# Layer norm 1 of the third batch applied as two rows to an already transposed x, and its Q products placed two blocks later

## The chip, the cores and the metric

The kernel runs on one core of a Trainium2 chip. The core has five engines with a queue of instructions each, executed in order: TensorE (PE, matrix products), VectorE (DVE), ScalarE (ACT), GpSimd (POOL) and SyncE (SP, which here only issues DMAs). They wait for one another through semaphores. The metric is the time of one execution on the device in microseconds (us); lower is better. Everything is float32.

## The reference

One transformer block with cross attention, for 4 batches of 512 query rows, 512 context rows, width 512, 16 heads of 32, and an MLP of width 2048. For each batch:

```
x  = layer_norm(hidden, ln1_w, ln1_b)                  # layer norm 1
q  = x @ q_w + q_b;  k = ctx @ k_w + k_b;  v = ctx @ v_w + v_b
a  = softmax(q k^T / sqrt(32), masked)  (per head)
h  = (a v) @ cproj_w + cproj_b + hidden
y  = layer_norm(h, ln2_w, ln2_b)                       # layer norm 2
out = h + gelu(y @ fc_w + fc_b) @ proj_w + proj_b
layer_norm(x, w, b) = (x - mean) * rsqrt(var + 1e-5) * w + b
```

The change concerns layer norm 1 of batch 2 (of batches 0 to 3) and the q products of its first two groups of heads.

## The kernel before

**Units and blocks.** The work on attention is cut into 16 units: unit w is batch w // 4 and four heads, group w % 4. A unit takes two blocks, one for each half of its query rows, so there are 32 blocks, p = 0 to 31, and block p belongs to unit p // 2. Batch 2 is units 8 to 11 and blocks 16 to 23. A block (`block`) has on PE the scores of its 256 query rows (L317), on DVE the mask and the row minimum of the scores (`soften`, L323), on ACT the exponential (L327), on DVE the 32x32 transposes of the result (`turn`, L335). Then comes the *exchange*: POOL copies the diagonal parts (L393, four copies) and SP issues twelve DMAs for the others (L398), into one buffer pT. The product with v (`attend`, L415) reads pT; DVE then multiplies by the reciprocal sums (L420), which frees pT for the exchange of the next block. From block 10 on, `attend` of block p - 2 stands at the start of block p, so each exchange has about one block to finish.

**Fills.** PE would be idle during a block's softmax, so other work is written into each block by hand: `put(p, ...)` lists it in order. `fill(0)`, `fill(1)` and `fill(2)` take pieces from the list at three places of a block, with a cost of 3.4 for a product over four chunks (K: `prep_k` L255; Q: `prep_q` L267; V: `prep_v` L278; output projection: `cproj` L455) and 0.0 for pieces that use no PE. A list given as `mid` is emitted in the middle of the block, between the softmax steps of its two 128-row halves. `some(2)` takes the next products of the MLP of batch 0, which starts in block 11. The order written there is the order on every engine; nothing reorders it.

**Layer norm 1, two ways.** For batches 0 and 2, x is loaded by rows (`load_x`), DVE takes the statistics (L129, L130), POOL works out the reciprocal deviations (`ln_rs`, L135 to L148), ACT normalizes for batch 2 (L153, key in `NORM_ACT`), PE transposes 16 blocks of 128x128 (`ln_turn`, L166), and ACT applies weight and bias while it moves the result from PSUM into `xT` (L171). For batches 1 and 3 (`BY_ROW`), the host supplies x transposed as well (`rawT`). The statistics come from x by rows as before, but the factor rs and the offset -mean * rs are turned into two rows: `store_rn` transposes a small tile on DVE (L203) and writes it to DRAM (four DMAs, L206), `load_rn` reads both rows back, spread over all partitions (two DMAs, L213), `ln1_rows` applies them to the transposed x on POOL (a multiply and an add for each of four 128x512 tiles, L218), and `ln1_affine` applies weight and bias on ACT into `xT` (L222).

**What stands around the change.** Block 9 has the output projection of batch 0 (`c`), with the statistics of layer norm 2 of batch 0 (`stat`) and its `ln_rs`. Block 10 normalizes it (`norm`; rows t = 0, 1, 2 on ACT, L153, and t = 3 on DVE, L157) and transposes it (`t2`, `ln2_turn`, L166). Block 11 has the first MLP product (`fc_seven`, L646). `fc_sums` makes weight sums for the MLP on POOL (four operations, L597 and L600, and two DMAs that POOL issues, L689 and L690), for one pair of weight tiles at a time; it stands in block 10 and, from p = 11 on, after `attend` at each block's start, and runs ahead of the products by at most two pairs. `pb_` adds a bias row on POOL (L426, four operations), `v_bias` another (L309).

Of the kernel before, what the change touches and what calls it, by code (L numbers as in the profile page):

```python
# [12 lines left out]
F32 = mybir.dt.float32  # L13
# [7 lines left out]
P = 128  # L21
# [14 lines left out]
IN_G = (1, 3, 5, 7)  # L36
IN_XE = (25, 27, 29, 31)

BY_ROW = ((1, 1), (1, 3))
BY_ACT = ((1, 2),)  # L40
NORM_ACT = BY_ACT + ((2, 0), (2, 1))
MW = 8
WARM = 9
PW = 2 * NT * HG * HD
# [7 lines left out]
def xattn_block(ctx: ExitStack, tc: tile.TileContext, x, rawT, encT, mask, q_w, k_w, v_w, c_w, fc_w, p_w, vecs, rows, out):  # L52
# [108 lines left out]
    def ln_turn(key, d, xn, dst):  # L161

        w, bi = (LN1W, LN1B) if key[0] == 1 else (LN2W, LN2B)
        tp = acc_tile(f"tp{key[0]}_{key[1]}_{d}")
        for t in range(NT):
            nc.tensor.transpose(tp[:, ts(t, P)], xn[t][:, ts(d, P)], ident)  # L166
        wd, bd = vec[:, w + d : w + d + 1], vec[:, bi + d : bi + d + 1]
        if d in (1, 2) and key not in BY_ACT:
            nc.vector.tensor_scalar(dst[:, d, :], tp, wd, bd, ALU.mult, ALU.add)
        else:  # L170
            nc.scalar.activation(dst[:, d, :], tp, AF.Identity, bias=bd, scale=wd)  # L171
# [23 lines left out]
            ln_rs((1, b))  # L195

    def load_raw(b):
        S["xn", b] = [tiles.tile([P, L], F32, tag="xn", name=f"raw_{b}_{d}") for d in range(ND)]
        for d in range(ND):
            nc.sync.dma_start(out=S["xn", b][d], in_=rawT[b, ts(d, P), :])  # L200

# [474 lines left out]
    def raw_pair(b, c):  # L676
        return [S["fcw", b, 2 * c + i] for i in range(2)]

    def fc_sums():

        while count[3] < len(fc_pairs) and count[3] < count[4] + 2:
            b, c = fc_pairs[count[3]]
            if ("fcw", b, 2 * c + 1) not in S:
                return
# [284 lines left out]
    def do(fn):  # L969
        return [(0.0, fn)]  # L970
# [104 lines left out]
    def stat(b, *ts_):  # L1075
        return do(lambda: [stat2(b, t) for t in ts_])
# [6 lines left out]
    def put(p, *work, before=(), mid=()):  # L1083

        work = [item for part in work for item in part]
        ahead[p], mids[p] = list(before), list(mid)
        fills[p] = work
# [15 lines left out]
    c, t2 = C(0), turns2(0)  # L1103
    put(7, [v6, k], cb(0))
    put(8, x1, [q, v], x4)
    put(9, c[:1], do(lambda: attend(3, 1)), x2[:2], c[1:2], x2[2:], stat(0, 0), c[2:3], stat(0, 1),
        c[3:], stat(0, 2), x3, stat(0, 3), rs(0))
    k, q, v = A(8)
    put(10, [k], norm(0, 0, 1), [v], norm(0, 2, 3), do(fc_sums), [q], t2)
    k, q, v = A(9)  # L1110
    put(11, [k, v], some(2), pb_(0), mid=do(lambda: y_sums(0)))

    x1, x2, x3, x4 = inputs(3)
    put(12, [q], some(2))
    k, q, v = A(10)
    put(13, [k], some(2))
    put(14, [q], some(2), x1)
    put(15, x2[:1], V(10), x2[1:2], do(lambda: load_raw(3)), some(2), do(lambda: store_rn(3)), some(1),
        do(lambda: load_rn(3)), some(1))
# [108 lines left out]
```

## Time and profile before

| what | us |
|---|---|
| median of 3 runs (lowest to highest) | 761.14 (760.96 to 763.58) |
| the profiled execution | 766.39 |
| its span, from first to last instruction | 764.3 |
| PE, busy | 757.5 (99%) |
| DVE, busy | 602.0 (79%) |
| ACT, busy | 337.1 (44%) |
| POOL, busy | 334.7 (44%) |

The profiled execution is 5.25 us longer than the median; 2.09 us of it lie outside the span. A line of the timeline has the start, the duration, engine, source line, operation, output and inputs, the count of instructions merged into it, and in brackets the idle time before it with what ended it. One product of the program over 512 columns shows as two MATMUL instructions.

### The profile page before, as it was taken

The page shows a single profiled execution, that of the slowest core. Times are in us where ns is not written, and L with a number is a line of the kernel's source. Part 1 is how long each engine was busy: PE and PEld are TensorE (multiplying, and loading weights), DVE is VectorE, ACT ScalarE, POOL GpSimd, SP SyncE. Part 2 cuts the span into 40 slices and gives each one's busy share as a digit, 9 for nine tenths or more (in the row PEclk, how much of TensorE's full clock was granted, in tenths as well). Part 3 has the DMA queues.
Part 4 walks back from the last instruction along what each step waited for, and adds up shares of the span by engine and source line. Part 5 has one row for each costly group of instructions (what it writes and reads, how often), then busy time and mean ns, then how long its engine had stood idle before and what let it go on. Part 6 is the DMA issues. An engine that isn't in the chain of part 4 may idle for free.

```text
span 764.3 us, 12899 instructions
## 1 busy us (share of the span) xinstructions
PE 757.5 (99%) x4370; PEld 518.7 (68%) x4370; DVE 602.0 (79%) x1198; ACT 337.1 (44%) x766; POOL 334.7 (44%) x350
## 2 busy tenths in 40 slices
PE   9999999999989999999999999999999999999998
PEld 6655555566565545475464566458888899988997
DVE  3888999879976777887888889958877886747762
ACT  2566766565863475647753467501202221021200
POOL 1539447368653883443584444532060004303152
PEclk9999999999999999999999999999999999999999
DMA  8999889467796686765666867776724402146001
GB/s 325 341 255 243 204 207 254 111 199 196 214 251 212 194 242 169 184 184 130 167 141 179 212 194 197 171 226 212 270 97 131 163 31 90 36 133 218 1 15 42
DMA packets 60577, 134.59 MB, mean 176 GB/s; under 512 B 11312, under 2 KB 17072, under 8 KB 60384
## 3 DMA queue, kind: packets, MB, share of 16 engines
q1 hardware_dynamic: 58448, 126.73, 58.0%
q0 software_dynamic: 1920, 7.01, 2.8%
q8 instruction: 35, 0.57, 0.3%
q14 instruction: 30, 0.25, 0.1%
q10 hardware_dynamic: 144, 0.02, 0.0%
HBM read 69.23 MB, written 11.02 MB: 105 GB/s over the span
## 4 chain that ended last, share of the span: by engine, by line
PE 98%; SPq 1%; DMA 1%; issue 0%; DVE 0%; POOL 0%; POOLq 0%; DVEq 0%
PE q L646 25%; PE accp L705 11%; PE r L790 8%; PE sc L317 8%; PE av L415 8%; PE acck L255 7%; PE accq L267 7%; PE accc L455 6%; PE accv L278 5%; PE accv L298 3%; PE q1p L844 2%; PE q4p L826 2%; PE tp L166 1%; SPq L398 1%; DMA ptt<-q_w_dram 1%; PE warm L1023 1%
## 5 line engine op out<-in xcount | busy, mean ns | idle before, releaser
L327 ACT ACTIVATE ptt<-ptt,mn 128x512 f32<-128x512 f32 x256 | 181.7, 711 | 147.6 <-DVE mn L323 147.6
L323 DVE CUSTOM_DVE_ANT_0 ptt<-sc,mb 128x512 f32<-128x512 f32 x256 | 160.6, 682 | 20.1 <-PE sc L317 20.0
L335 DVE STREAM_TRANSPOSE tb<-ptt 128x1024 f32<-128x1024 f32 x128 | 153.3, 1217 | 1.0 <-ACT ptt L327 1.0
L393 POOL COPY pT<-tb 32x1088 f32<-32x1088 f32 x96 | 104.5, 1089 | 86.4 <-DMA pbt<-p_w_dram 28.0
L705 PE MATMUL accp<-pbt,gt 128*128 128x512 f32 x192 | 85.3, 596 | 0.0
L646 PE MATMUL q<-yT,gt 128*128 128x256 f32 x320 | 78.9, 380 | 0.0
L667 ACT ACTIVATE ga<-ga,vec 128x512 f32<-128x512 f32 x40 | 26.7, 714 | 93.3 <-DVE ga L600 83.5
L646 PEld LDWEIGHTS q<-yT,gt 128*128 128x128 f32 x320 | 61.0, 191 | 8.1
L705 PEld LDWEIGHTS accp<-pbt,gt 128*128 128x128 f32 x192 | 35.9, 190 | 44.6 <-issue 39.2
L317 PE MATMUL sc<-pbt 32*128 32x512 f32 x512 | 66.1, 621 | 0.0
L646 PE MATMUL q<-ys,gt 128*128 128x256 f32 x240 | 61.6, 380 | 0.0
L255 PE MATMUL acck<-xe,ptt 128*128 128x512 f32 x128 | 58.8, 603 | 0.2 <-issue 0.2
L267 PE MATMUL accq<-xe,ptt 128*128 128x512 f32 (+1 forms) x136 | 58.5, 575 | 0.0
L646 PEld LDWEIGHTS q<-ys,gt 128*128 128x128 f32 x240 | 45.7, 191 | 6.1
L600 DVE TENSOR_TENSOR ga<-q,ga 128x512 f32<-128x512 f32 (+1 forms) x60 | 36.2, 603 | 16.9 <-PE q L646 14.3
L415 PE MATMUL av<-pT,v 128*32 128x256 f32 x768 | 47.3, 387 | 2.0 <-DMA ptt<-q_w_dram 2.0
L327 ACT ACTIVATION_READ_ACCUMULATOR ptt<-ptt,mn 128x1 f32 x256 | 47.8, 187 | 0.0
L267 PEld LDWEIGHTS accq<-xe,ptt 128*128 128x128 f32 x136 | 24.9, 190 | 31.4 <-issue 23.0
L317 PEld LDWEIGHTS sc<-pbt 32*128 32x128 f32 x512 | 27.5, 187 | 26.0 <-issue 17.2
L255 PEld LDWEIGHTS acck<-xe,ptt 128*128 128x128 f32 x128 | 23.6, 192 | 31.2 <-issue 21.9
L455 PE MATMUL accc<-wc,oT 128*128 128x512 f32 x96 | 42.5, 598 | 0.0
L415 PEld LDWEIGHTS av<-pT,v 128*32 128x32 f32 x768 | 23.0, 111 | 26.2 <-issue 10.4
(219 smaller groups left out, 1265.4 us busy)
## 6 DMA issues: line engine op xcount, KB each, us to landing
pT<-tb SPq DMA_DIRECT2D x288, 136.0 KB, 2.4
pbt<-p_w_dram SPq DMA_DIRECT2D x40, 256.0 KB, 3.3
gt<-ws SPq DMA_DIRECT2D x20, 512.0 KB, 3.4
gt<-tb SPq DMA_DIRECT2D x48, 136.0 KB, 3.8
xe<-tb SPq DMA_DIRECT2D x48, 136.0 KB, 2.5
pbt<-fc_w_dram SPq DMA_DIRECT2D x24, 256.0 KB, 4.0
gt<-fc_w_dram SPq DMA_DIRECT2D x20, 256.0 KB, 3.2
ptt<-k_w_dram SPq DMA_DIRECT2D x16, 256.0 KB, 3.7
```

The lines of the kernel that those rows point to most:

```text
L255: nc.tensor.matmul(acc, S["wk", w][:, d, :], eT[:, d, :], start=(d == 0), stop=(d == ND - 1))
L267: nc.tensor.matmul(acc, S["wq", w][:, d, :], xT[:, d, c], start=(d == 0), stop=(d == ND - 1))
L317: nc.tensor.matmul(S["sc", w, qt][h], qT[r, ts(qt, P)], kT[r, :], start=True, stop=True)
L323: nc.vector.tensor_tensor_reduce(out=s, in0=S["sc", w, qt][h], in1=S["mb", w // NG], scale=1.0, scalar=FMAX, op0=ALU.add, op1=ALU.min, acc ...
L327: nc.scalar.activation(s, s, AF.Exp, bias=mn, scale=-1.0, accum_out=S["sums", w][:, qt, h : h + 1])
L335: nc.vector.transpose(tv[:, qt % 2, 2 * k : 2 * k + 2], S["ps", w, qt, k])
L393: nc.gpsimd.tensor_copy(pT[ts(i, HD), i], tb[ts(i, HD), i])
L415: nc.tensor.matmul(av[ts(h, HD), : 2 * P].rearrange(shape, **kw), v[:, t, ts(h, HD)], p[t][h], start=(t == 0), stop=(t == NT - 1),)
L455: nc.tensor.matmul(acc, S["oT", b][:, g, ts(t, P)], wc[:, g, :], start=(g == 0), stop=(g == NG - 1))
L646: nc.tensor.matmul(o, x[:, k], y[:, k], start=(k == 0), stop=(k == 1))
L705: nc.tensor.matmul(acc, gT[q % 2][:, k, ts(t, P)], S["pw", b, q * FQ + k], start=(k == 0), stop=(k == FQ - 1))
L790: nc.tensor.matmul(r, x[:, c], w[:, c], start=(c == 0), stop=(c == NP // 2 - 1))
```

## The change

Batch 2 joins `BY_ROW`: its x is loaded transposed as well, straight into `xT`, and the two rows and then weight and bias are applied there in place. The normalization on ACT, the 16 transposes on PE and the four moves from PSUM on ACT go away for batch 2. `load_raw(2)`, `store_rn(2)` and `load_rn(2)` stand in block 9; `ln1_rows(2, ...)` is split, tiles 0 and 1 in block 10 and tiles 2 and 3 in block 11, each time behind the copies of that block's exchange in POOL's queue; `ln1_affine(2)` ends block 11. Since `xT` is complete only then, Q of unit 8 moves from block 10 to block 12, and Q of unit 9 from block 12 to block 13. In block 10, `fc_sums` makes one pair instead of two (the second then comes at the start of block 11), the normalization of t = 0, 1 of layer norm 2 moves to the middle of the block, and that of t = 2, 3 ahead of V.

```diff
-BY_ROW = ((1, 1), (1, 3))
-BY_ACT = ((1, 2),)
-NORM_ACT = BY_ACT + ((2, 0), (2, 1))
+BY_ROW = ((1, 1), (1, 2), (1, 3))
+NORM_ACT = ((2, 0), (2, 1))
...
-        if d in (1, 2) and key not in BY_ACT:
+        if d in (1, 2):
...
     def load_raw(b):
-        S["xn", b] = [tiles.tile([P, L], F32, tag="xn", name=f"raw_{b}_{d}") for d in range(ND)]
+        S["xn", b] = [
+            xT[:, d, :] if b == 2 else tiles.tile([P, L], F32, tag="xn", name=f"raw_{b}_{d}") for d in range(ND)
+        ]
...
-    def fc_sums():
+    def fc_sums(ahead=2):
 
-        while count[3] < len(fc_pairs) and count[3] < count[4] + 2:
+        while count[3] < len(fc_pairs) and count[3] < count[4] + ahead:
...
-    put(9, c[:1], do(lambda: attend(3, 1)), x2[:2], c[1:2], x2[2:], stat(0, 0), c[2:3], stat(0, 1),
-        c[3:], stat(0, 2), x3, stat(0, 3), rs(0))
-    k, q, v = A(8)
-    put(10, [k], norm(0, 0, 1), [v], norm(0, 2, 3), do(fc_sums), [q], t2)
-    k, q, v = A(9)
-    put(11, [k, v], some(2), pb_(0), mid=do(lambda: y_sums(0)))
+    put(9, c[:1], do(lambda: attend(3, 1)), x2[:2], do(lambda: load_raw(2)), c[1:2], do(lambda: store_rn(2)), stat(0, 0),
+        c[2:3], stat(0, 1), do(lambda: load_rn(2)), c[3:], stat(0, 2, 3), rs(0))
+    k, q8, v = A(8)
+    put(10, [k], do(lambda: ln1_rows(2, 0, 1)), norm(0, 2, 3), [v], do(lambda: fc_sums(1)), t2, mid=norm(0, 0, 1))
+    k, q9, v = A(9)
+    put(11, [k], do(lambda: ln1_rows(2, 2, 3)), [v], some(2), pb_(0), do(lambda: ln1_affine(2)),
+        mid=do(lambda: y_sums(0)))
...
-    put(12, [q], some(2))
+    put(12, [q8], some(2))
     k, q, v = A(10)
-    put(13, [k], some(2))
+    put(13, [k, q9], some(2))
```

## The prediction

> **What bounds the kernel now.** I read the page first (busy times, then the chain that ended last), next the waits of PE, then the timeline of each engine over blocks 9 to 15.
>
> ```profile
> span 764.3 us, 12899 instructions
> PE 757.5 (99%) x4370; PEld 518.7 (68%) x4370; DVE 602.0 (79%) x1198; ACT 337.1 (44%) x766; POOL 334.7 (44%) x350
> PE 98%; SPq 1%; DMA 1%; issue 0%; DVE 0%; POOL 0%; POOLq 0%; DVEq 0%
> ...
> PE av L415 <- DMA ptt<-q_w_dram: 2.0, 1, 2.0
> ```
>
> PE is busy for 757.5 of 764.3 us and is 98% of the chain. So a microsecond of PE work taken away is a microsecond gained, if no wait takes its place; and work that other engines gain or lose costs nothing until PE waits for it. Inside the stream PE waits once for long: 2.0 us ahead of a product with v, at the start of block 15. The stretches around it, with the clock in the column behind the counts, show that this wait has a tail.
>
> ```profile
> 220.00:222.00 2.00, 1.83 (x28) 1.32 (x32) 0.21 (x1) 0.94 (x1) 0.00 (x0) 0.78 1.01 354
> 222.00:224.00 2.00, 2.00 (x19) 0.69 (x15) 0.42 (x1) 0.00 (x0) 0.47 (x1) 0.50 1.01 380
> 224.00:226.00 2.00, 2.00 (x18) 0.81 (x11) 1.16 (x3) 0.43 (x1) 1.92 (x3) 0.87 0.84 236
> ```
>
> The granted clock is 0.78, 0.50 and 0.87 there, so 2 x (0.22 + 0.50 + 0.13) = 1.70 us of PE's work are lost. A wait of 2 us thus cost 3.7 us. That sets the price of every new wait below.
>
> The blocks around the change, on PE:
>
> ```profile
> 142.42 1.91 PE L166 MATMUL tp<-ident,xn 128*128 128x128 f32 x16
> 144.26 1.93 PE L415 MATMUL av<-pT,v 128*32 128x256 f32 x32
> 151.59 3.74 PE L278 MATMUL accv<-ptt,xe 128*128 128x128 f32 x32
> 155.16 3.60 PE L267 MATMUL accq<-xe,ptt 128*128 128x512 f32 x8
> 158.60 2.14 PE L166 MATMUL tp<-ident,xn 128*128 128x128 f32 x16
> 160.67 1.93 PE L415 MATMUL av<-pT,v 128*32 128x256 f32 x32
> 177.71 1.93 PE L415 MATMUL av<-pT,v 128*32 128x256 f32 x32
> 191.18 1.93 PE L415 MATMUL av<-pT,v 128*32 128x256 f32 x32
> 220.17 2.77 PE L415 MATMUL av<-pT,v 128*32 128x256 f32 x32 [1.98 <-DMA ptt<-q_w_dram]
> ```
>
> Each `av` row is a block's start: block 10 at 144.26, 11 at 160.67, 12 at 177.71, 13 at 191.18, 15 at 220.17. Below I give times of the new kernel on this same clock.
>
> **Part 1: sixteen transposes leave PE (end of block 9).** They hold PE from 142.42 to 144.26: -1.84 us. PE's projection before them still ends at 142.42, so block 10 starts there.
>
> **Part 2: what else leaves and comes in block 9.** ACT loses four normalizations and four moves and gains four `ln1_affine`; SP gains four loads, four stores and two reads; DVE gains one small transpose.
>
> ```profile
> 139.20 2.93 ACT L153 ACTIVATE xn<-xn,nm,rs 128x512 f32<-128x512 f32 x4 [0.42 <-POOL nm L148]
> 240.28 0.20 DVE L203 STREAM_TRANSPOSE rnT<-rn 128x32 f32<-128x32 f32 x1
> 240.51 1.30 SPq L206 DMA_DIRECT2D rn<-rnT  x4
> 242.73 0.82 SPq L213 DMA_DIRECT2D rn<-rn  x2
> DMA to landing us min/median/max: 3.5/3.9/4.3
> ```
>
> The ACT work was hidden (no PE row waited for it but the transposes that go). For the rows, batch 3's chain gives the price: from DVE's transpose at 240.28 to the end of the reads' issue 3.3 us, and the L213 line gives at most 4.3 us to landing, together 7.6 us. In block 9 the transpose can stand at about 140.4, behind an addition of the projection, so the rows are there by 148.0; POOL first asks for them at 151.5 (part 4). Cost 0, with 3.5 us of cover. SP is through with the ten DMAs by 143.6, ahead of the next exchange, which it issues from 145.4; without that cover each late microsecond would be one of the exchange.
>
> **Part 3: block 10 without Q.** Q of unit 8 took 158.60 - 155.16 = 3.44 us of PE here. It is not saved, it moves to block 12, and Q of unit 9 moves on to block 13; the sum of both is 0. But it was the cover behind which ACT normalized layer norm 2 of batch 0 for the transposes at 158.60.
>
> ```profile
> 153.83 0.69 DVE L323 CUSTOM_DVE_ANT_0 ptt<-sc,mb 128x512 f32<-128x512 f32 x1
> 153.95 0.72 ACT L327 ACTIVATE ptt<-ptt,mn 128x512 f32<-128x512 f32 x1 [1.59 <-DVE mn L323]
> 155.38 0.66 ACT L257 ACTIVATE pbt<-acck,vec 128x512 f32<-128x512 f32 x1
> 155.94 1.51 ACT L153 ACTIVATE xn<-h,nm,rs 128x512 f32<-128x512 f32 x2
> 158.12 0.82 ACT L153 ACTIVATE xn<-h,nm,rs 128x512 f32<-128x512 f32 x1
> ```
>
> In the new order ACT has: four exponentials, normalization of t = 0 and 1 (1.51 us, which fit its idle 1.59 us ahead of 153.95), four more exponentials, of which the last two are held by DVE as here until 155.38, the move of K (0.56 to the next start), then t = 2 (0.82). Counted from the block's start as here, t = 2 is ready at 155.38 + 0.56 + 0.82 = 156.76. PE ends V at 155.16, does the two transposes it can (2 x 0.115) and stands until about 156.8: a new wait of 1.4 us. The 14 others take 1.61 us, so the next block starts at 158.45 against 160.67 - 3.44 = 157.23 if nothing waited: +1.22 us (the 0.23 us by which the row at 158.60 exceeds the one at 142.42 is in it). From below the term is -0.23 (no wait at all), from above +3.3 (t = 2 as late as in the row at 158.12). I take 1.22, since the rows of ACT and DVE that give it are those of the same block and only change places. Block 11 then starts at 158.45 - 1.84 = 156.61.
>
> The exchange begun in block 10 must also be in by then:
>
> ```profile
> 145.01 0.19 POOL L135 TENSOR_SCALAR ve<-mv 128x4 f32<-128x4 f32 x1 [5.84 <-DVE mv L130]
> 146.77 8.44 SPq L398 DMA_DIRECT2D pT<-tb  x12
> ...
> pT<-tb SPq DMA_DIRECT2D x288, 136.0 KB, 2.4
> ```
>
> DVE ends its statistics at 145.0 (POOL's row), as now, and then frees pT, so SP starts at about 145.4, 1.3 us earlier. The last of the twelve is issued by 153.3 and lands 2.4 us later, at 155.7: hidden, with 0.9 us of cover ahead of 156.61.
>
> **Part 4: POOL's queue.** Here the change puts the most behind other work: eight operations, and they stand ahead of copies that PE needs.
>
> ```profile
> 147.00 4.47 POOL L393 COPY pT<-tb 32x1088 f32<-32x1088 f32 x4
> 159.74 0.73 POOL L600 TENSOR_TENSOR wsum<-pbt 128x256 f32<-128x256 f32 x1
> 164.28 0.74 POOL L600 TENSOR_TENSOR wsum<-pbt 128x256 f32<-128x256 f32 x1
> 166.60 1.05 POOL L597 TENSOR_TENSOR wsum<-pbt,wsum 128x256 f32<-128x256 f32 x1
> 176.55 1.26 POOL L309 TENSOR_TENSOR v<-v,row 128x512 f32<-128x512 f32 x1 [2.81 <-ACT v L283]
> 177.77 4.97 POOL L426 TENSOR_TENSOR h<-h,row 128x512 f32<-128x512 f32 x4
> 182.69 4.47 POOL L393 COPY pT<-tb 32x1088 f32<-32x1088 f32 x4
> 253.49 10.38 POOL L218 TENSOR_TENSOR raw<-raw,rn 128x512 f32<-128x512 f32 x8
> ```
>
> A pair of `fc_sums` with its two DMA issues is 164.28 - 159.74 = 4.54 us, half of the rows 10.38 / 2 = 5.19. The first copies stay at 147.00, since they stand behind `ln_rs`, which starts at 145.01 in both kernels. From there POOL has no gap: copies 4.47, rows 5.19 (to 156.66), v_bias 1.26, one pair 4.54 (to 162.46), copies of block 11's exchange 4.47, the second pair 4.54 (to 171.5), rows 5.19 (to 176.66), v_bias 1.26, `pb_` 4.92, and the copies of block 12's exchange end at 187.3 (now 182.69 + 4.47 = 187.16). PE asks for them at the start of block 13: 156.61 + 17.04 (177.71 - 160.67) + 13.47 (191.18 - 177.71) = 187.12. So block 13 waits some 0.2 us, with a semaphore's passage 0.3 us: +0.3. From below it is 0; from above, if every row operation is stretched like the one at 166.60 (1.05 for 0.73), 8 x 1.30 x 0.44 = 4.6 us more.
>
> Who waits for the rows: `ln1_affine` ends at about 177.4, Q of unit 8 starts 3.8 us into block 12, at 177.45, and needs the fourth tile 2.6 us later. ACT's exponentials behind it start then too. Cost 0. Block 13, 3.5 us longer with Q of unit 9, lets POOL catch up; from block 14 on the order is as before.
>
> **Sum.** -1.84 + 1.22 + 0.3 = -0.3 us: 764.0 us of span, 766.1 for such a profiled execution. The median shown is 5.25 us under the profiled time; I carry the difference over to it: 761.14 - 0.3 = 760.8.
>
> **Rivals.**
>
> *A, the clock drops in block 10.* The new wait of 1.4 us is shorter than the 1.98 us that halved the clock, and transposes stand beside it. If it suffices: -0.3 + 1.70 = +1.4, 762.5. Against it: no drop at 158.60, with 2.07 us of transposes and a short wait; for it: from the end of V to the next product with v 3.3 us pass here.
> The Trainium skill, "TensorE: Matmul & The Clock Gate", Part 1 and Part 4, says that the gate watches free-running windows of about 3.4 us and that transposes don't count as busy; by that the whole 3.3 us would be idle, and the drop would hang on the window's phase. The trace has full clock at both rows of transposes but none as long, so it doesn't settle this.
>
> *B, slower: POOL becomes the bound.* The rows stretch as in the upper bound of part 4; block 13 waits 4.9 us and the clock drops: -1.84 + 1.22 + 4.9 + 1.7 = +6.0, 767. It decides (over +3.8) once POOL is some 2.5 us later than I count. For it: the chain of part 4 has no slack at all. Against: the stretched row at 166.60 ran beside DVE sums on two SBUF inputs, and beside the rows DVE has mainly scores from PSUM.
>
> *C, block 15's wait goes.*
>
> ```profile
> 207.16 8.52 SPq L398 DMA_DIRECT2D pT<-tb  x12
> 215.08 0.56 POOL L689 DMA_DIRECT2D ws<-wsum  x1 [0.30 <-POOL wsum L597]
> 215.64 0.54 POOL L690 DMA_DIRECT2D ws<-pbt  x1
> ```
>
> The last exchange DMA goes out at the same moment as POOL's two, and PE waits. Block 13 is now longer and has one more weight load, so SP and POOL may meet otherwise: -0.3 - 1.98 - 1.70 = -4.0, 757.1. For it: it needs a shift of only half a microsecond, and single runs between 760.96 and 763.58 look as if such waits come and go. Against: block 14's own order is the same, and a wait that the unprofiled runs don't have can't be won.
>
> *D, the change doesn't do what it says*: the rows come late and Q of unit 8 waits; the cover of 2.6 us and more in parts 2 and 4 speaks against it.
>
> **How the numbers follow.** Forecast 0.50 (its own range 759 to 762), A 0.21, B 0.12, C 0.13, D and other losses 0.04. Range 757.0 to 764.5: it holds all but B and D. About 0.5% or 3.8 us is what a measurement of this kernel can tell from no change. Faster by more: C, 0.12. Slower by more: B and D, 0.15. Within: 0.73.
>
> **What would show it.** No L166 rows at block 9's end; the transposes of block 10 in two pieces with 1.2 to 1.6 us between them; a POOL queue without a gap from block 10's copies to block 12's; block 13's `av` released by POOL; Q of unit 8 with no idle ahead. Wrong would make it: a clock under 1.0 at block 11 (A), over 2 us ahead of block 13's `av` (B), no idle ahead of block 15's (C).

## The result: 767.2 us, slower, and outside the predicted range

The changed kernel took 767.21 us (median of 12 executions, 763.67 to 768.99) against 761.74 us for the kernel before (12 executions, 760.93 to 763.93). The medians are 5.47 us apart; the ratio that the measurement gives, which is not their quotient, is 1.0051, with a 95% interval of 1.0038 to 1.0065. The forecast was 760.8, its range 757.0 to 764.5. The profiled execution is the longest of the twelve, 768.99 us. First its page: span, busy times and the chain of work that ended last.

```profile
span 767.2 us, 12885 instructions
PE 758.2 (99%) x4354; PEld 517.7 (67%) x4354; DVE 603.7 (79%) x1199; ACT 334.1 (44%) x762; POOL 345.9 (45%) x358
PE 93%; DVE 2%; DMA 2%; SPq 1%; issue 1%; POOL 0%; ACT 0%; DVEq 0%; POOLq 0%
```

PE has 16 matrix instructions fewer, the transposes (4354 for 4370), and is not less busy, and only 93% of the chain is PE's, where it was 98%. The other 5%, some 38 us, are not idle time of PE: at a wait the chain leaves PE and follows what was waited for, above all from 160.03 back to 126.96 through an exchange and DVE's work ahead of it, while PE was busy with other things. What PE lost by waiting stands in its waits by line (total, times, longest):

```profile
PE av L416 <- DMA pT<-tb: 3.6, 2, 2.0
PE tp L165 <- ACT xn L152: 0.9, 1, 0.9
```

On PE's timeline, the starts of blocks 10 to 13 and 15 and what lies between (start, duration, operation, idle time before):

```profile
143.70 1.93 PE L416 MATMUL av<-pT,v 128*32 128x256 f32 x32
154.97 0.38 PE L165 MATMUL tp<-ident,xn 128*128 128x128 f32 x2
156.24 1.75 PE L165 MATMUL tp<-ident,xn 128*128 128x128 f32 x14 [0.89 <-ACT xn L152]
160.03 2.76 PE L416 MATMUL av<-pT,v 128*32 128x256 f32 x32 [2.03 <-DMA pT<-tb]
180.57 2.58 PE L318 MATMUL sc<-pbt 32*128 32x512 f32 x16
192.75 1.93 PE L416 MATMUL av<-pT,v 128*32 128x256 f32 x32
224.81 1.93 PE L416 MATMUL av<-pT,v 128*32 128x256 f32 x32 [1.62 <-DMA pT<-tb]
```

The transposes of block 10 are in two pieces, as foretold, with 0.89 us between them. Block 11 then waits 2.03 us for an exchange that was to be hidden. Block 13 (192.75) doesn't wait for POOL, whose copies end at 185.75 + 4.48 = 190.2:

```profile
185.75 4.48 POOL L394 COPY pT<-tb 32x1088 f32<-32x1088 f32 x4
```

Block 12's scores (180.57) take 2.58 us for 2.00, and block 10's (at 145.57) take 2.37: PE comes to them earlier, DVE's last statistics of block 9 (L129) end at 146.11, and by the trace three of the sixteen products start only then. The windows behind block 11's start show the clock in the column behind the counts:

```profile
160.00:162.00 2.00, 1.98 (x28) 1.35 (x32) 0.00 (x0) 0.00 (x0) 1.84 (x4) 0.75 0.01 4
162.00:164.00 2.00, 2.00 (x16) 0.79 (x12) 0.42 (x1) 0.00 (x0) 1.70 (x4) 0.50 0.12 46
164.00:166.00 2.00, 2.00 (x14) 0.58 (x11) 1.31 (x5) 0.57 (x1) 1.96 (x2) 0.90 0.91 284
```

2 x (0.25 + 0.50 + 0.10) = 1.70 us of PE's work are lost to the halved clock. Why the exchange is late stands in SP's timeline (start, time in which the DMAs are issued, count) and in the chain of waits (start, duration to landing):

```profile
139.93 2.02 SPq L201 DMA_DIRECT2D xe<-rawT_dram  x4
142.05 1.30 SPq L207 DMA_DIRECT2D rn<-rnT  x4
146.35 0.82 SPq L214 DMA_DIRECT2D rn<-rn  x2
147.28 7.83 SPq L399 DMA_DIRECT2D pT<-tb  x12
```

```profile
147.84 5.44 DMA pT<-tb
153.88 5.57 DMA pT<-tb
```

The four stores of the rows (L207) go out behind 1 MB of raw tiles (L201), and SP holds the two reads (L214) until the stores have landed, from 143.35 to 146.35. The exchange follows at 147.28 behind 0.5 MB of broadcast reads. By the landings in the trace its first DMA takes 5.3 us to land, where it took 2.3 in the kernel before. It issues a DMA about every 0.63 us, a little slower than they land, so the delay shrinks slowly: 4.4 us are left at the eighth, and the last three, behind a gap in the landings, take 5.3 to 5.6. The eighth to the tenth wait for the DMA eight places ahead of each to land: 147.84 + 5.44 = 153.28, and the tenth goes out at 153.30.

### The profile page after: what moved, and what is told of

Read it like the earlier page. It is cut to its first block, busy times and chain, and to the rows that moved or that the text cites. A ratio compares the mean times of both kernels' runs of the same rounds, so it can differ in the third digit from the quotient of the medians.

```text
span 767.2 us, 12885 instructions
## 1 busy us (share of the span) xinstructions
PE 758.2 (99%) x4354; PEld 517.7 (67%) x4354; DVE 603.7 (79%) x1199; ACT 334.1 (44%) x762; POOL 345.9 (45%) x358
## 4 chain that ended last, share of the span: by engine, by line
PE 93%; DVE 2%; DMA 2%; SPq 1%; issue 1%; POOL 0%; ACT 0%; DVEq 0%; POOLq 0%
PE q L647 24%; PE accp L706 11%; PE r L791 8%; PE sc L318 8%; PE av L416 7%; PE acck L256 7%; PE accq L268 7%; PE accv L279 4%; PE accc L456 4%; PE accv L299 3%; PE q1p L845 2%; PE q4p L827 2%; DMA pT<-tb 2%; SPq L399 1%; PE tp L165 1%; DVE st L128 1%
## 5 line engine op out<-in xcount | busy, mean ns | idle before, releaser
L328 ACT ACTIVATE ptt<-ptt,mn 128x512 f32<-128x512 f32 x256 | 181.7, 711 | 154.4 <-DVE mn L324 154.4
L318 PE MATMUL sc<-pbt 32*128 32x512 f32 x512 | 68.1, 622 | 0.0
```

Of the source, the lines that this page charges most:

```text
L318: nc.tensor.matmul(S["sc", w, qt][h], qT[r, ts(qt, P)], kT[r, :], start=True, stop=True)
L328: nc.scalar.activation(s, s, AF.Exp, bias=mn, scale=-1.0, accum_out=S["sums", w][:, qt, h : h + 1])
```

## The blocks, side by side

The table gives, for one profiled execution of each kernel, the time from the start of a block's scores to that of the next block's, worked out from the timelines; a wait ahead of a block's product with v thus stands in the row of the block before. Blocks 0 to 8 together differ by up to 2.5 us between these executions, whatever the kernel (block 2 takes 10.86 to 12.15, block 4 10.99 to 12.66); block 15 takes 24.63 where the clock is full, and from block 16 on all agree within 0.2 us.

| kernel | 9 | 10 | 11 | 12 | 13 | 14 | sum |
|---|---|---|---|---|---|---|---|
| before, first profile | 21.53 | 16.41 | 17.04 | 13.47 | 13.47 | 16.36 | 98.28 |
| e1 before again | 21.53 | 16.42 | 17.04 | 13.47 | 13.47 | 13.47 | 95.40 |
| changed | 19.79 | 17.14 | 17.85 | 14.05 | 16.90 | 15.16 | 100.89 |
| e9 changed again | 19.79 | 15.21 | 17.04 | 15.20 | 16.90 | 13.47 | 97.61 |
| e2 moves only | 21.53 | 14.22 | 17.04 | 15.21 | 16.90 | 13.47 | 98.37 |
| e3 rows only | 19.79 | 16.54 | 17.04 | 14.64 | 13.47 | 13.47 | 94.95 |
| e4 no read | 19.79 | 14.22 | 17.04 | 14.97 | 16.90 | 15.20 | 98.12 |
| e5 loads split | 19.79 | 14.22 | 17.04 | 14.94 | 16.90 | 18.17 | 101.06 |
| e6 sums back | 19.79 | 18.39 | 17.04 | 14.95 | 16.90 | 13.47 | 100.54 |
| e7 norm early | 19.78 | 16.42 | 17.90 | 14.63 | 16.90 | 17.34 | 102.97 |
| e8 all three | 19.79 | 14.20 | 17.04 | 15.33 | 16.90 | 14.96 | 98.21 |
| e10 one input | 19.78 | 14.21 | 17.04 | 13.77 | 16.90 | 14.79 | 96.49 |
| e11 split, norm | 19.79 | 13.90 | 17.04 | 15.20 | 16.90 | 13.47 | 96.30 |
| e12 Y on GpSimd | 19.79 | 13.45 | 17.04 | 17.10 | 16.90 | 13.47 | 97.75 |
| e13 bias later | 19.79 | 14.49 | 17.04 | 13.62 | 16.90 | 17.43 | 99.27 |
| e14 (before) bias later | 21.53 | 16.41 | 17.91 | 13.47 | 13.47 | 13.47 | 96.25 |
| e15 (e11) sums late | 19.79 | 13.64 | 17.04 | 15.38 | 16.90 | 16.44 | 99.20 |
| e16 (e13) sums late | 19.79 | 13.80 | 17.04 | 13.66 | 16.90 | 15.39 | 96.58 |
| e17 (before) sums late | 21.53 | 16.41 | 17.04 | 13.47 | 13.47 | 13.47 | 95.39 |
| e18 sums in 15 | 19.78 | 13.45 | 17.04 | 13.89 | 16.90 | 13.47 | 94.53 |

Block 9 gains 1.74 us in every kernel without the transposes. Q costs nothing by being moved: 16.90 - 13.47 = 3.43 us in block 13, and nearly as much less in block 10 (e12, e18: 13.45 with a wait of 0.27 and scores of 2.37 us). The rest of the changed kernel's row is loss, in three places: block 10 (with its clock in block 11), block 12, block 14.

## The experiments

**e1 and e9: each kernel again.** A single profile of each had left open which waits are fixed parts.

> The kernel before, unchanged, for a second profile. The question is whether the wait ahead of block 15 with its halved clock (1.98 + 1.70 us in the first profile, which took 766.39 us against a median of 761.7) belongs to the kernel or to that one execution. If to the execution: no wait over 0.5 us ahead of block 15's product with v and a profiled time near 762. If to the kernel: a wait of 1.5 to 2 us there again, 764 to 766.

Measured: 763.0 us, ratio 0.9992 (0.997 to 1.0014). Block 15's wait of 1.98 us, which stood in the first profile of the kernel before, is absent: it comes and goes.

> The changed kernel once more, unchanged, for a second profiled execution. In its first profile TensorE waits 2.03 us ahead of block 11 and its clock is halved for 3.41 us from there. If that wait is a fixed part of the change (theory): it is there again, 1.5 to 2.5 us, and the step from block 10 to 11 takes 16.4 to 18.5 us; runs whose mean clock is 0.998 take some 2.5 to 3 us more than those at 1.0, and the median is 765 to 767.5. Rival, it belonged to the one execution: no wait above 0.5 us ahead of block 11 and a median of 764 or less.

Measured: 766.87 us (12 executions, 762.14 to 769.36), ratio 1.0036 (1.0014 to 1.0058). PE's timeline and the chain of waits of this execution:

```profile
153.37 1.75 PE L165 MATMUL tp<-ident,xn 128*128 128x128 f32 x14 [0.89 <-ACT xn L152]
156.04 1.93 PE L416 MATMUL av<-pT,v 128*32 128x256 f32 x32 [0.92 <-DMA pT<-tb]
174.94 3.73 PE L318 MATMUL sc<-pbt 32*128 32x512 f32 x16
```

```profile
139.81 3.33 DMA rn<-rnT
143.68 5.44 DMA rn<-rn
150.96 4.46 DMA pT<-tb
```

The wait for the exchange is there again, at 0.92 us and with a full clock; the wait for ACT is 0.89 as before, and block 12's scores take 3.73 us. The exchange's wait is a part of the change whose size varies. Over all executions the mean clock tells how often it was halved somewhere: it is 0.998 or less in 11 of 24 of the changed kernel, in 19 of the 159 of the kernel before that ran beside the experiments. Above that the changed kernel's medians are 764.99 (7 executions) and 765.0 (6), at 0.998 or less they are 767.99 (5) and 768.04 (6).

**e2 and e3: one part of the change each.**

```diff
 e2 (kernel before; layer norm 1 of batch 2 still by transposes)
-    put(10, [k], norm(0, 0, 1), [v], norm(0, 2, 3), do(fc_sums), [q], t2)
+    put(10, [k], norm(0, 2, 3), [v], do(lambda: fc_sums(1)), t2, mid=norm(0, 0, 1))
-    put(12, [q], some(2))
+    put(12, [q8], some(2))
-    put(13, [k], some(2))
+    put(13, [k, q9], some(2))
 e3 (changed kernel; Q of units 8 and 9 where they were)
-    put(10, ... do(lambda: fc_sums(1)), t2, mid=norm(0, 0, 1))
+    put(10, ... do(lambda: fc_sums(1)), [q8], t2, mid=norm(0, 0, 1))
```

> Only the moves: Q of units 8 and 9 in blocks 12 and 13, the new order of block 10; layer norm 1 of batch 2 stays on its transposes. Theory R (the rows' reads, issued by SP right ahead of block 10's exchange, hold it up): no wait for the exchange ahead of block 11, a wait of about 0.9 us inside block 10's transposes, 0.5 to 1.5 us slower than before. Rival C (block 10 without Q is too short for any exchange): a wait of 1.5 us or more ahead of block 11 with a halved clock, 3 us or more slower than before.

> The changed kernel with Q of units 8 and 9 back in blocks 10 and 12, where they read the transposed context in place of xT, since that is not complete there; so the values of q of units 8 and 9 are wrong and the amount of work is the same. Theory R: the exchange of block 10 still lands some 5 us after issue in place of 2.4, but Q (3.4 us) covers it; no wait ahead of block 11, and the 1.84 us of transposes come out as a gain of about 1.5 us. Rival C: the exchange lands 2.4 us after issue with Q there, and the gain is the same. A rival P (POOL's rows delay block 13) would show a wait of 1 us or more ahead of block 13 released by POOL.

Measured: e2 765.84 us, ratio 1.0033 (1.002 to 1.0047); e3 764.08 us, 1.0022 (1.0006 to 1.0038). Block 11's start in each, on PE:

```profile
158.06 1.75 PE L166 MATMUL tp<-ident,xn 128*128 128x128 f32 x14 [1.25 <-ACT xn L153]
159.73 1.93 PE L415 MATMUL av<-pT,v 128*32 128x256 f32 x32
```

```profile
154.96 3.60 PE L269 MATMUL accq<-xe,ptt 128*128 128x512 f32 x8
160.23 1.93 PE L417 MATMUL av<-pT,v 128*32 128x256 f32 x32
```

Neither waits for the exchange. In e2 block 10 is short and no rows are read; in e3 the rows are read, the exchange's first DMA takes 3.2 us to land, and Q's 3.6 us stand in front of the exchange's consumer. So that wait needs both halves of the change: the one delays the exchange, the other takes away the work behind which it would have been late unseen. Block 12 loses in both (15.21, 14.64 for 13.47), which neither theory held, and so e3's gain of 1.5 us did not come: its blocks add up to 0.45 us less than e1's, and its median lies above the kernel before's.

**e4 and e5: what delays the exchange.** e4 leaves out the two reads, e5 puts two of the four raw tiles behind block 10's exchange.

```diff
 e4
     def load_rn(b):
+        if b == 2:
+            S["rows", b] = S["rows", 1]
+            return
 e5
-    do(lambda: load_raw(2)), c[1:2]
+    do(lambda: load_raw(2, (0, 1))), c[1:2]
-    put(11, ...)
+    put(11, ..., before=do(lambda: load_raw(2, (2, 3))))
```

> The changed kernel without the two reads that spread the rows of batch 2: it applies the rows of batch 1, which still lie in their tiles, so layer norm 1 of batch 2 is wrong; every other instruction stays. Theory R: block 10's exchange lands 2.4 us after issue, the wait of 2.03 us ahead of block 11 and the halved clock go, 3 to 4 us faster than the changed kernel (763 to 764). Rival C: the wait ahead of block 11 stays at 1.5 us or more, the time stays at 767.

> The changed kernel, but only two of the four raw tiles of batch 2 are loaded in block 9; the other two at the start of block 11, behind the exchange of block 10. If the four loads delay the stores of the rows, these the reads, and the reads the exchange of block 10 (theory): the stores land within some 2.5 us instead of 3.1 to 3.6, the reads go out before 145 instead of at 146.35 (times from the changed kernel's span), the matmuls on the weights of block 9's second half find their data, and the step from block 10 to 11 takes 14.2 (if no wait is left there but that of the transposes) to 15 us in place of 17.14, with the clock at full speed: 2.5 to 4.5 us less than the changed kernel, about 763.5. Rival, the two broadcast reads load the DMA engines whatever goes ahead of them: the wait ahead of block 11 stays at 1.5 to 2.5 us and the time at 766 to 767. The 0.9 us on the layer norm's third tile and block 12's 0.6 us stay in both.

Measured: e4 766.03 us, ratio 1.0023 (1.0004 to 1.0041); e5 765.94 us, 1.0029 (1.0008 to 1.005). SP and PE in e5:

```profile
140.24 1.30 SPq L208 DMA_DIRECT2D rn<-rnT  x4
142.47 0.82 SPq L215 DMA_DIRECT2D rn<-rn  x2
145.38 7.49 SPq L400 DMA_DIRECT2D pT<-tb  x12
```

```profile
156.48 1.93 PE L417 MATMUL av<-pT,v 128*32 128x256 f32 x32
```

The stores land in 1.2 us for 3.1 to 3.6, the reads go out 0.93 us behind the last store for 3.0, and by the landings in the trace the first ten DMAs of the exchange take 2.3 to 2.4 us, as they do in e4. Neither kernel waits ahead of block 11, and block 10 takes 14.22 us. In the six kernels with the reads and all four loads in block 9 (changed, e3, e6, e7, e9, e10) the exchange's first DMA takes 3.2 to 5.5 us; in the nine with the reads left out or the loads split (e4, e5, e8, e11, e12, e13, e15, e16, e18) it takes 2.3. The delay is the reads', and through them the raw loads'. What is left is a gap near the exchange's end: in those nine kernels the eleventh DMA lands in 3.6 to 4.6 us. Its cause stays open; in e8 PE still waits 1.02 us for the exchange ahead of block 11. The totals, forecast at 763 to 764, don't show the repair, since block 12 still loses and block 15's wait, 1.67 us in e4 and 2.93 in e5, came on top.

**e6, e7, e8: the other two losses.** e6 makes both pairs of weight sums in block 10 again, e7 normalizes the third tile in the middle of the block, e8 joins e5, e6 and e7.

```diff
 e6
-    do(lambda: fc_sums(1)), t2
+    do(fc_sums), t2
 e7
-    norm(0, 2, 3), [v], ... mid=norm(0, 0, 1)
+    norm(0, 3), [v], ... mid=norm(0, 0, 1, 2)
```

> The changed kernel, but both pairs of weight sums are made in block 10, as in the kernel before. If block 12's loss (its first scores to those of block 13: 14.05 to 15.21 us in the three kernels with one pair in block 10, 13.47 before) comes from the sums on GpSimd lying beside VectorE's four sums of Y at the start of block 11 (theory): the sums of Y take 0.9, 1.0, 0.7 and 0.7 us again, and block 12 takes 13.47. Rival, it comes from the row operations' place on GpSimd or from another queue: block 12 stays at 14 or more. The wait ahead of block 11 stays (2.0 us and a halved clock), so the total changes by 0.6 to 1.7 us only: 765 to 766.5; but GpSimd's copies for block 11 start 3.6 us later, at 167.5, and end at 172.5, ahead of their matmuls at 178.7: no new wait.

> The changed kernel, but the third tile of layer norm 2 of batch 0 is normalised with the first two, between the two groups of exponentials of block 10, instead of behind them all. If TensorE's wait of 0.89 us ahead of the transposes is for that one operation of ScalarE (theory): the wait is gone, and the step from block 10 to 11 is shorter by 0.5 to 0.9 us unless the wait ahead of block 11, which ends with a landing, grows by as much; that one then reads 2.5 to 2.9 us and the total stays at 766.5 to 767.5. Rival, the exponentials behind it are 0.75 us later, the last transposes of VectorE with them, and the exchange behind: block 11's wait grows by more than 0.9, total 768.

> The three edits of the runs beside this one together (two raw tiles behind the exchange of block 10, both pairs of weight sums in block 10, the third tile normalised early). If the three causes named are the whole of the loss: the blocks 9 to 13 take 19.8, 13.5, 17.0, 13.5 and 16.9 us, no wait ahead of block 11 and none ahead of the transposes, and the kernel takes what the kernel before takes less the 1.8 us of transposes: 760.5 to 761.5 with no wait ahead of block 15, 762 to 763.5 with one (it comes and goes: 1.7 us with its halved clock at twice that). Rival, another thing is in the changed blocks that the three do not touch: 764 or more with a step above those named.

Measured: e6 767.16 us, ratio 1.004 (1.0014 to 1.0066); e7 764.7 us, 1.0028 (0.9999 to 1.0057); e8 766.29 us, 1.0024 (1.0003 to 1.0046). In e7 the transposes stand in one piece and the 0.89 us are gone; 0.44 of them come back in the wait for the exchange (2.47 for 2.03), and block 10 takes 16.42 us for 17.14:

```profile
152.69 1.91 PE L165 MATMUL tp<-ident,xn 128*128 128x128 f32 x16
157.07 2.71 PE L416 MATMUL av<-pT,v 128*32 128x256 f32 x32 [2.47 <-DMA pT<-tb]
```

e6 refutes its theory: block 12 takes 14.95. DVE's sums of Y (L598) and POOL's work beside them, in e6:

```profile
168.61 1.57 DVE L598 TENSOR_TENSOR yT<-yT 128x512 f32<-128x512 f32 x1
170.10 1.57 DVE L598 TENSOR_TENSOR ys<-yT,ys 128x512 f32<-128x512 f32 x1
```

```profile
167.03 5.60 POOL L394 COPY pT<-tb 32x1088 f32<-32x1088 f32 x4
```

It is now POOL's copies (5.60 us for 4.47) that lie beside the sums, and both are stretched. In e1 the same sum of DVE, beside POOL's DMA issues, took 0.68:

```profile
167.90 0.68 DVE L597 TENSOR_TENSOR yT<-yT 128x512 f32<-128x512 f32 x1
```

So it is not the weight sums alone (beside them e1's first two sums took 0.94 and 1.03): POOL's copies stretch DVE more. The four sums hold DVE for 5.3 us in e6 (from 166.31 to its next instruction at 171.60) and 3.2 in e1; its last additions from PSUM then end at 181.7, behind PE's product with v (177.88 to 179.81), and PE's scores of block 12 wait for them: by the trace two of the sixteen products start 0.04 to 0.05 us behind DVE's last addition and its multiplication, in e6 (181.73, 182.06) as in the changed kernel (181.65, 181.98), and none does in e1. The next run tests the cause. e8 keeps block 12's loss (15.33) and shows the limit on the other side: with the sums moved, POOL's copies are 1.16 us late ahead of block 13.

**e10: that contention.** DVE's four two-input sums are replaced by four transposes of the same size.

```diff
-        sub(ys[:, 0], y12, y11) ... sub(ys[:, 2], y21, ys[:, 1], e)
+        for o, i in ((ys[:, 0], y12), (ys[:, 1], y22), (y12, y22), (ys[:, 2], y21)):
+            nc.vector.transpose(o, i)
```

> The changed kernel, but VectorE's four sums of Y in block 11 (two inputs in SBUF each) are replaced by four transposes of one input of the same size, so the MLP of batch 0 gets other numbers; nothing else is changed. In five kernels the sums took 1.0 to 1.6 us each where they lay beside work of GpSimd (its copies, its weight sums) and 0.68 alone. If block 12's loss is this contention (theory): the four transposes take 0.6 to 0.7 us each beside the same GpSimd work, GpSimd's copies of block 11 take 4.5 us and its weight sums 0.73 each, VectorE is through with block 11 some 1.5 to 3 us earlier, and block 12 takes 13.47 us instead of 14.05 to 15.3. Rival, VectorE is late for another reason (block 11's start, the order of its products): block 12 stays at 14 or more.

Measured: 765.36 us, ratio 1.0012 (0.9988 to 1.0036). DVE, POOL and PE:

```profile
161.61 1.30 DVE L623 STREAM_TRANSPOSE ys<-yT 128x512 f32<-128x512 f32 x2
```

```profile
162.07 4.50 POOL L394 COPY pT<-tb 32x1088 f32<-32x1088 f32 x4
```

```profile
175.04 2.00 PE L318 MATMUL sc<-pbt 32*128 32x512 f32 x16
186.95 1.93 PE L416 MATMUL av<-pT,v 128*32 128x256 f32 x32 [0.19 <-POOL pT L394]
```

With one input the same POOL work lies beside DVE and neither is stretched: 0.65 us for a transpose, 4.50 for the copies, scores at 2.00, block 12 at 13.77, of which 0.19 is the wait ahead of block 13. The contention is shown. The Trainium skill, "SBUF — State Buffer", section "Who interferes with whom", says that a DVE instruction with two SBUF inputs contends with a GpSimd instruction that reads SBUF; by these rows it does.

**e11, e12, e13, e14: repairs.** e11 joins e5 and e7. e12 adds two of the four sums of Y on POOL, with the second pair of weight sums behind them. e13 puts the row operations of block 11 ahead of that pair and moves the projection's bias additions, `pb_(0)`, from block 11 to block 13. e14 puts the two sums of Y on POOL and `pb_(0)` in block 13 in the kernel before. The diff shows only these two edits.

```diff
 e12
-        e = nc.gpsimd if b == SPLIT else nc.vector
+        e = nc.gpsimd
 e13, e14
-    put(11, ... some(2), pb_(0), ...)
+    put(11, ... some(2), ...)
-    put(13, [k, q9], some(2))
+    put(13, [k, q9], some(2), pb_(0))
```

> The changed kernel with two raw tiles loaded behind the exchange of block 10 and the third tile normalised early, and one pair of weight sums in block 10 as in the change: the two edits that took a wait away each, without the third, which took nothing away. By what the single runs showed: block 9 takes 19.79, block 10 13.0 to 14.2 (a wait of up to 1.2 us for the exchange may be left, as in the run with all three), block 11 17.04, block 12 14.6 to 15.3, block 13 16.9. Against the kernel before, whose blocks 9 to 13 take 21.53, 16.42, 17.04, 13.47 and 13.47: between 0.6 us less and 1.4 more, so 762.5 to 764.5. Rival, the waits come back elsewhere (block 12 behind GpSimd's copies, block 15 behind the weight sums' stores): 765 or more.

> The kernel with two raw tiles behind the exchange and the early third tile, and beside it two of the four sums of Y on GpSimd, behind its copies and ahead of the second pair of weight sums. If block 12's loss is VectorE's being late by the contention (theory): VectorE has 2.3 to 3 us less in block 11, block 12 takes 13.47 to 14 us, and the kernel takes 761 to 763: at the kernel before or up to 0.2% below it. Rival, GpSimd has no room left: its copies for block 12 end 2 us later or more, TensorE waits for them ahead of block 13, or the products of the first pair wait for GpSimd's sums of Y: 764 or more.

> The changed kernel with two raw tiles behind the exchange, the early third tile, two of the four sums of Y on GpSimd, the row operations of block 11 ahead of the second pair of weight sums, and the projection's four bias additions (4.97 us of GpSimd) in block 13 instead of block 11. If the three causes are the whole loss (theory): GpSimd's copies for block 12 end some 5 us earlier than in the run with the sums alone, ahead of their matmuls; blocks 9 to 13 take 19.8, 13.0 to 13.9, 17.0, 13.5 and 16.9 us, together with block 14's 13.47 some 94.2 against 95.4 in the kernel before, and the kernel takes 761 to 762.5. Rival, GpSimd is the bound of these blocks whatever the order: a wait for its copies of 1 us or more ahead of block 13, 14 or 15, 764 or more.

> The kernel before, with two of the four sums of Y on GpSimd and the projection's bias additions in block 13. In it block 12 takes 13.47 us already and VectorE waits for TensorE at the head of blocks 11 and 12, so both edits should give nothing if they only mend what the change broke (theory): 762 to 764, blocks 9 to 14 as before. Rival, they shorten a block of the kernel before as well: 761.5 or less, and a gain of the run beside this one is not the change's.

Measured: e11 763.23 us, ratio 1.0004 (0.9981 to 1.0027); e12 769.9 us, 1.0069 (1.0047 to 1.009); e13 766.28 us, 1.0022 (1.0001 to 1.0044); e14 763.78 us, 1.0001 (0.9983 to 1.0019). PE in e12:

```profile
174.02 2.00 PE L319 MATMUL sc<-pbt 32*128 32x512 f32 x16
189.26 1.93 PE L417 MATMUL av<-pT,v 128*32 128x256 f32 x32 [2.56 <-POOL pT L395]
```

e11 takes two losses away and stands level with the kernel before. In e12 block 12's scores are at 2.00 and POOL is the bound: the prediction's rival B, with 2.56 us, once POOL has 2.6 us more to do; and Q of unit 8 waits 0.69 us for `ln1_affine`, a small piece of rival D. In e13 both waits are gone and block 12 takes 13.62, but its profile has block 15's wait (2.31 us), 7 of 12 executions have a clock of 0.998 or less, and the median misses its forecast of 761 to 762.5. e14's blocks 12 to 14 stay at 13.47 and its block 11 takes 17.91 for 17.04, with a wait of 0.60 for the sums of Y on POOL: the edits gain nothing there, so what they mend is the change's own damage.

**e15 to e18: block 15's wait.** The stores of POOL's weight sums go out near block 14's last exchange DMA. e15 (e11), e16 (e13) and e17 (kernel before) write the sums of block 14 at its end, e18 (e13) leaves them to block 15, so that it has the first half of this diff alone.

```diff
-        if p > 10:
+        if p > 10 and p != 14:
             fc_sums()
-    put(14, [q], some(2), x1)
+    put(14, [q], some(2), x1, do(fc_sums))
```

> The changed kernel with two raw tiles behind the exchange and the early third tile, and GpSimd's weight sums of block 14 at the end of that block's work instead of at its head, so that their two stores go out behind the last exchange transfer. If the stores make block 15's wait (theory): no wait above 0.5 us ahead of block 15, that transfer lands within 2.6 us, block 14 takes 13.47 to 14, and of 12 executions at most two have a mean clock of 0.998 or less; median 762.5 to 764. Rival, the wait comes from the gap of some 2 us in the landings a few transfers earlier: it stays in about as many executions, median as in the run without this edit or above.

> The kernel with the bias additions in block 13 and two of the sums of Y on GpSimd, with the same edit in block 14. It had a mean clock of 0.998 or less in 7 of 12 executions, and a wait of 2.3 us ahead of block 15 in its profile. By the theory: that wait is gone, blocks 9 to 14 take 94 to 95.5 us against 95.4 in the kernel before without its wait, at most two executions with the clock halved, median 761.5 to 763.5. Rival, as in the run beside it: the wait stays, 765 or more.

> The kernel before with the same edit in block 14 alone. Its first profile has the wait (1.98 us and a halved clock), a later one does not, and the mean clock is 0.998 or less in 16 of 113 executions. By the theory: no such execution or one, no wait ahead of block 15, and the upper end of its times (766 to 767.8) is gone, median 762 to 763, ratio 0.997 to 1.0. Rival: nothing changes in either.

> The kernel with the bias additions in block 13 and two of the sums of Y on GpSimd, with GpSimd's weight sums of block 14 left to block 15, so that no store of theirs goes out while block 14's exchange does. By the theory (the stores make block 15's wait): no wait ahead of block 15, its last exchange transfer lands within 2.6 us, at most one of 12 executions with a mean clock of 0.998 or less, and a median of 761 to 763, at or below that of the kernel before with its own stores late (762.44). Rival, the later exchange of block 14 alone is enough for the wait: 1 us or more is left ahead of block 15, or the wait moves to a later block; 764 or more.

Measured: e15 765.39 us, ratio 1.0028 (1.0009 to 1.0047); e16 764.63 us, 1.0012 (0.9992 to 1.0031); e17 762.44 us (761.11 to 764.18), 0.9978 (0.9962 to 0.9994); e18 761.77 us (759.69 to 763.51), 0.9989 (0.9977 to 1.0002). In e15 (2.24 us) and e16 (1.85 us) the wait stays. The reason is that the edit didn't move the stores: POOL makes these sums right behind the same four copies either way, and the first store goes out 8.55 to 8.58 us after the start of block 14's scores in e11, e13, e15 and e16. The same holds for e1 (scores at 206.27) and e17 (at 207.16):

```profile
214.84 0.56 POOL L689 DMA_DIRECT2D ws<-wsum  x1 [0.30 <-POOL wsum L597]
```

```profile
215.74 0.56 POOL L689 DMA_DIRECT2D ws<-wsum  x1 [0.30 <-POOL wsum L597]
```

So the edit of these three runs shows nothing of the stores. That e17's ratio lies 0.22% below 1 and none of its 12 executions has a clock of 0.998 or less (3 of 29 of the kernel before beside it) isn't shown to come from them. POOL and PE of e15:

```profile
216.39 0.56 POOL L691 DMA_DIRECT2D ws<-wsum  x1 [0.30 <-POOL wsum L599]
```

```profile
221.74 2.60 PE L417 MATMUL av<-pT,v 128*32 128x256 f32 x32 [2.24 <-DMA ptt<-q_w_dram]
```

The exchange's last DMA goes out at 216.49 and lands 5.0 us later. In e18, without a store in block 14, it lands 2.4 us after its issue, all 12 executions have a clock of 1.0 where e13 had 7 of 12 at 0.998 or less (of the kernel before beside them 0 of 17 and 5 of 23), and PE's waits on the page come to this:

```profile
PE av L417 <- DMA pT<-tb: 0.6, 2, 0.3
```

The twenty traces (the first of each kernel and e1 to e18) show the rest. In ten of them (before, changed, e4, e5, e7, e8, e10, e13, e15, e16) POOL's first store goes out before the last exchange DMA or at most 0.11 us behind it; there that DMA takes 3.8 to 5.1 us to land, and PE waits 1.3 to 2.9 us ahead of block 15. In nine (e1, e2, e3, e6, e9, e11, e12, e14, e17) the store is 0.26 us or more behind it; there it takes 2.9 us at 0.26 and 2.5 or less from 0.6 on, and PE doesn't wait. The store's moment is nearly fixed, so SP's decides: from the first issue of this exchange to the last it takes 7.8 to 8.6 us in the ten and 7.2 to 7.7 in the nine. That the stores are what slows it, and not the later moment, shows in SP's next two DMAs, weights of 256 KB: issued 8.6 to 9.7 us after the start of the scores, they take 3.7 to 5.1 us to land in the nine and 3.2 in e18, without stores. So the meeting with the stores makes block 15's wait; what slows SP in some executions stays open.

e18, the change with the causes found here mended, takes 94.53 us for blocks 9 to 14 against 95.40 in e1, but its ratio to the kernel before can't be told from 1. Nothing here shows e18 to be better than e17, which ran beside other executions of the kernel before.

## Why the prediction was wrong

- *Part 1* held: 1.74 us less in block 9, for 1.84. That PE then comes to block 10 ahead of DVE's statistics was not counted; its scores take 2.37 us there for 2.00.
- *Part 2 failed*, at "Cost 0, with 3.5 us of cover. SP is through with the ten DMAs by 143.6". The changed kernel runs 1.28 us later there (block 10's first product at 143.70 for 142.42), so 143.6 is 144.9 on its clock; SP was through at 147.17, 2.3 us later. The price was taken from batch 3's chain, where SP stands still for 0.92 us between the stores and the reads (241.81 to 242.73); behind four raw loads it stands still for 3.00. What the loads and the reads leave in the queue for the exchange behind them was in no term.
- *Part 3's second half failed with it, and here the time was lost*: "lands 2.4 us later, at 155.7: hidden, with 0.9 us of cover" is 157.0 on the new clock; the exchange landed at 159.83, 2.8 us late, and PE waited 2.03 (0.92 in e9). The issue was only 0.5 us late (done at 155.11 for 154.6); the landing took 5.3 us for 2.4. The 2.4 us were taken as a constant, and they are one only where nothing is queued ahead and no gap comes (e4, e5: 2.3 to 2.4 for ten DMAs, 3.7 to 4.1 for the last two).
- *Part 3's first half* came out by luck in part. A wait of 1.4 us for ACT was foretold and 0.89 measured; the term, +1.22, is 14.22 - (16.42 - 3.43) = +1.23 us in e4 and e5, where PE doesn't wait for the exchange, because the scores' 0.37 us make up for most of the difference.
- *Part 4 held for what it counted*. Where no earlier wait pushes PE back, in e10, block 13 waits 0.19 us for POOL's copies; "some 0.2 us" was said. No run shows the 0.1 us for a semaphore's passage: in e10 PE starts 0.06 us behind the end of the copies (182.42 + 4.47 = 186.89, 186.95). In the changed kernel the copies end at 190.2 and PE asks at 192.75.
- *A term was missing*: block 12, +0.58 and +1.73 us in the two profiles. Rival B weighed that POOL is stretched beside DVE's sums of two SBUF inputs (the row at 166.60), as a matter of POOL's room alone. That DVE is stretched as well, and that PE waits for DVE, was not asked (e10). Without it, and with no wait for the exchange, the sum holds: e10's blocks 9 to 13 take 81.70 us for 81.93 in e1, 0.23 less for a forecast of 0.3.
- *Rival A* had the right price, 1.70 us, and the wrong place: the clock fell after the exchange's wait, not after the transposes'.
- *Rival B's* 767 is the measured time by chance. Its mechanism is real (e8, e12), but not in this kernel.
- *Rival C*: the wait went in e9 and stayed in the first profile. The meeting of the stores with the last exchange DMA, which it named, is its cause (e18 and the twenty traces); what it missed is that the kernel before has the wait in some of its executions only, so the median had little of it to win.

In sum, against e1: the changed kernel's first profile is -1.74 + 1.23 (the late norm and the scores of block 10) + 2.03 and 1.70 (the exchange and its clock) + 0.58 (block 12) + 1.69 (block 14) = +5.49 us, and e9's is -1.74 + 1.23 + 0.99 + 1.73 = +2.21; the medians, 5.47 and 3.58 us apart (3.9 and 2.8 by the ratios), lie between.

## What to carry to other kernels

When a step adds small DMAs that wait for each other, price them in the queue they join: what is issued ahead of them sets when they land, and the transfers behind them start from that backlog and, if they are issued at nearly the rate at which they land, lose it slowly. When two edits each look free, ask whether the one spends the cover of the other; here the moved Q was what hid the late exchange. When a row shows one engine stretched beside another, look whether the other is too, and who waits for each. And look in the trace whether an edit moved what it was to move: three of these did not.

## What the runs showed of the hardware

- *The clock has a grid.* In the traces of all these kernels the stretches of full and of halved clock are, but for the last of each, multiples of 3.413 us (153.6 = 45, 215.04 = 63, 218.45 = 64 of them), counted from the start of the first full one, and a halved stretch is one of them, two in e5. In these traces it hangs on how much of one such window PE stands idle whether the next is halved: 0.58 or more did so in eight cases (before 0.58, changed 0.60, e7 0.62, e13 0.63, e15 0.65), 0.56 or less did not (e12's 2.56 us, split 0.56 and 0.19 over two windows; e16's 1.85 us, 0.46). e5's second halved window doesn't fit: PE is idle for 0.26 of the one before it. The Trainium skill, "TensorE: Matmul & The Clock Gate", section "Part 1: The HAM clock gate (the "warmup" mystery)", says that the window is 3413 ns and free-running; the traces agree. That section asks for a whole idle window, and here 0.58 of one was enough.
- *Transposes kept the clock up.* In e2 the wait of 1.25 us and 14 transposes fill 0.86 of one window, and the clock stayed full; had they counted as idle, it should have fallen (e9's 0.89 us and its transposes fill as much, with a full clock). The Trainium skill, "TensorE: Matmul & The Clock Gate", section "Part 4: PE-mode transpose", says that they don't count as busy in the same way; for these f32 transposes both runs speak against counting them as idle.
- *POOL's stores delay SP's DMAs*: beside the two stores of weight sums (128x768 and 128x256 f32) the last exchange DMA landed 4.4 to 5.1 us after its issue (changed, e5, e7, e13, e15) for 2.4 (e18); issued 0.26 us ahead of the first store it took 2.9 (e12), 0.6 us ahead 2.5 (e1).
- *A backlog on SP's queue shrinks slowly*: DMAs of 136 KB, one every 0.63 us, land in 2.3 to 2.4 us from an empty queue (e5); behind 0.5 MB of reads they went from 5.3 to 4.4 us over eight DMAs (changed) and from 4.0 to 2.9 over ten (e10).
- *DVE and POOL stretch each other*: 1.57 us for 0.68 and 5.60 for 4.47 (e6).
